# The order of the rows and the cut of the stores in a pairwise outer-product kernel with batch normalisation

## The chip, the cores and the metric

The kernel runs on one core of one Trainium2 chip, alone. The metric is the device time of one execution in microseconds (us). All data are float32. A kernel of this chip writes instructions for several engines, each of which works through its own list in order: PE (TensorE, matmuls), DVE (VectorE), ACT (ScalarE), POOL (GpSimd) and SP (SyncE, which here only issues transfers). Transfers between the device memory (HBM) and the on-chip memory (SBUF, 128 partitions) are carried by 16 DMA engines that take them in the order of issue. Engines wait for each other and for transfers by semaphores.

## The reference: what is computed

There are 1024 samples, 39 fields and 16 values per field. For each pair of fields (r, c) with c < r, 741 pairs in all, the outer product of field r of xj with field c of xi is formed, normalised over the batch, and weighted:

```python
cross = xj[:, rows, :, None] * xi[:, cols, None, :]          # 1024 x 741 x 16 x 16
mean = jnp.mean(cross, axis=(0, 2, 3), keepdims=True)
var = jnp.mean(jnp.square(cross - mean), axis=(0, 2, 3), keepdims=True)
normed = (cross - mean) * jax.lax.rsqrt(var + BN_EPS)
normed = normed * gamma[None, :, None, None] + beta[None, :, None, None]
out = normed[:, :, None, :, :] * W[None, None, :, :, :]
```

The pairs stand in the order of `tril_indices`: row r holds the r pairs (r, 0) to (r, r-1). The inputs are small (5.1 MB). The output is 1024 x 741 x 256 values, 776.99 MB, and all of it must be written.

## The kernel before, in words

**Layout.** Each of the 128 partitions holds eight samples. A tile is one row r for T = 2 of these eight samples, so each row has four tiles (t0 = 0, 2, 4, 6). In the buffer `y_sb` one pair of one sample takes 256 values, 1 KB per partition. `y_sb` has room for 152 such places, that is two halves of 76. A row r from 20 to 37 and its partner 38 - r fill one half together, r pairs for two samples and then 38 - r pairs for two samples; row 38 fills one alone; row 19 fills half of one. Inside a tile the first sample's pairs come first, then the second's (`view`, L135). "Sample 0" and "sample 1" below are these two. Successive halves of work go to the two halves of the buffer in turn (`slot`, L68 to L74), so a half is overwritten by the half after next.

**Order.** The list `tiles` (L67 to L74) fixes the order of the work: four tiles of row 19, then for r = 20, 21, ... 37 the tiles r and 38 - r in turn for the four values of t0, and at the end the four tiles of row 38. Tile number n below is the place in this list: n = 0 to 3 are row 19, 4 to 11 are rows 20 and 18.

**Statistics.** The first 33 us or so load the inputs and work out a scale and a shift for each pair. They are then spread to all partitions by matmuls (`spread`, L475, matmuls at L482), group of rows by group of rows into banks of PSUM, and joined with gamma and beta by three or four small DVE operations per group (`apply`, L491 to L500). ROW_GROUPS (L32) lists for each group its rows, its bank and the tile n after which it is applied. All matmuls are issued before the main loop.

**Main loop (L516).** For tile n: POOL scales xi for tile n + 2 (`scale_xi`, L161; L167); `finish(n)`; the groups that are due; `products(n + 1)`. `products` (L175) writes the raw products of a tile with one instruction per sample and value i of 16: sample 0's sixteen first, then sample 1's. Eleven or twelve of each sixteen are ACT's (L145), the other four or five POOL's (L147). Rows up to SHORT = 4 are made by DVE (L180, L190) from a copy of xj in PSUM, `xj_short`, that ACT makes once (L526). Each product writes all pairs of its sample, so no pair is complete before the last of them. `finish` (L247) then adds the shift and multiplies by W: one DVE instruction per pair for both samples (L284), while for some pairs POOL does it (L270, L273); in rows over LONG = 33 that is eight pairs, and ACT does the addition for them (L268).

**Stores.** `finish` calls `store` (L203) after each piece of pairs that `bounds` (L240) gives: one piece for rows up to ONE = 24, two of r//2 and r - r//2 pairs for longer ones, and a written-out list for the first eight tiles. A store is issued by SP, which waits for the engines that finish the pairs. For a row over ONE the last piece goes out as two stores, one per sample; every other store takes both samples. In each partition a store moves one contiguous run per sample. Rows 25 to 38 thus have three stores per tile, the first of which takes the first half of the pairs of both samples.

Of the kernel before, what the change touches and what calls it, by code (L numbers as in the profile page):

```python
# [14 lines left out]
T = 2  # L15


ONE, LONG = 24, 33
FIRST_PIECES = (
    (0, 1, 3, 6, 10, 14, 19), (0, 4, 9, 14, 19), (0, 4, 11, 19), (0, 9, 19), (0, 10, 20), (0, 9, 18), (0, 10, 20), (0, 9, 18)  # L20
)
# [8 lines left out]


ROW_GROUPS = (  # L32
    (19, 20, 0, None), (20, 21, 1, None), (15, 19, 1, 2), (21, 25, 2, 4), (1, 15, 2, 8), (25, 32, 3, 16), (32, 39, 4, 24)
)
SHORT_GROUP = 4


@with_exitstack
def tile_pair_outer_batchnorm(
# [17 lines left out]
    NB, F, E = xi.shape  # L57
# [8 lines left out]
    mid = (F - 1) // 2  # L66
    tiles = [(mid, t0, t0 // T * half // 2) for t0 in range(0, NT, T)]  # L67
    slot = 0  # L68
    for r in range(mid + 1, F):
        for t0 in range(0, NT, T):  # L70
            tiles.append((r, t0, slot * half))
            if r < F - 1:
                tiles.append((F - 1 - r, t0, slot * half + T * r))
            slot ^= 1  # L74
# [60 lines left out]
    def view(n):  # L135
        r, _, u = tiles[n]
        return y_sb[:, u : u + T * r, :].rearrange("p (t n) e -> p t n e", t=T)
# [23 lines left out]
    def scale_xi(n):  # L161
        r, t0, _ = tiles[n]
        if r <= SHORT:
            return
        n0 = first[r]
        xs = scaled.tile([P, T, r, E], F32, tag="xs", name=f"xs_{r}_{t0}")
        nc.gpsimd.tensor_tensor(  # L167
            xs,
            xi_sb[:, t0 : t0 + T, 0:r, :],
            s_sb[:, :, n0 : n0 + r, :].to_broadcast([P, T, r, E]),  # L170
            ALU.mult,
        )
        xs_of[n] = xs

    def products(n):  # L175

        r, t0, _ = tiles[n]
        if r <= SHORT:
            xs = scaled_short.tile([P, T, r, E], F32, tag="xs_short", name=f"xs_{r}_{t0}")
            nc.vector.tensor_tensor(  # L180
                xs,
                xi_sb[:, t0 : t0 + T, 0:r, :],
                s_short[:, first[r] : first[r] + r]
                .unsqueeze(1)
                .unsqueeze(3)
                .to_broadcast([P, T, r, E]),
                ALU.mult,
            )
            for t in range(T):
                nc.vector.tensor_tensor(  # L190
                    view(n)[:, t].rearrange("p n (i j) -> p n i j", j=E),
                    xs[:, t].unsqueeze(2).to_broadcast([P, r, E, E]),
                    xj_short[:, t0 + t, r - 1 : r, :].unsqueeze(3).to_broadcast([P, r, E, E]),
                    ALU.mult,
                )
            return
        xs = xs_of.pop(n)
        split = E - (POOL_I_FIRST[n] if n < 3 else POOL_I_LONG if tiles[n][0] > LONG else POOL_I)
        for t in range(T):
            for i in range(E):  # L200
                product(n, nc.scalar if i < split else nc.gpsimd, t, i, xs[:, t])

    def store(n, c0, c1, t_from=0, t_to=T):  # L203
        r, t0, _ = tiles[n]
        n0 = first[r]

        step = 1 if r > ONE and c1 == r else t_to - t_from
        for t in range(t_from, t_to, step):
            nc.sync.dma_start(  # L209
                out_v[:, t0 + t : t0 + t + step, (n0 + c0) * EE : (n0 + c1) * EE],  # L210
                view(n)[:, t : t + step, c0:c1, :].rearrange("p t n e -> p t (n e)"),
            )
# [14 lines left out]
    def weigh(n):  # L227

        y = view(n)
        for c0, c1 in zip(bounds(n), bounds(n)[1:]):  # L230
            affine(n, range(c0, min(c1, OWN)), (nc.vector,))
            nc.vector.tensor_tensor(  # L232
                y[:, :, c0:c1, :],
                y[:, :, c0:c1, :],
                w_dve.unsqueeze(1).to_broadcast([P, T, c1 - c0, EE]),
                ALU.mult,
            )
            store(n, c0, c1)
# [8 lines left out]
    def finish(n):  # L247


        r = tiles[n][0]  # L250
        n0 = first[r]
        y = view(n)
        long = r > LONG
        p1 = r // 2 if long else r
        if long:
            share = POOL_PAIRS_LONG
        elif RAW < n < 10:
            share = POOL_PAIRS_FIRST
        else:
            share = int(r * POOL_SHARE + 0.5) if r > SHORT else 0  # L260
        p0 = p1 - share
        step = POOL_PAIRS_LONG // 2 if long else r
        for c0 in range(p0, p1, step):
            c1 = min(c0 + step, p1)
            for c in range(c0, c1):
                t_c = t_sb[:, n0 + c : n0 + c + 1]
                if long:
                    nc.scalar.activation(y[:, :, c, :], y[:, :, c, :], AF.Identity, bias=t_c)  # L268
                else:
                    nc.gpsimd.tensor_scalar(  # L270
                        y[:, :, c, :], y[:, :, c, :], t_c, 1.0, ALU.add, ALU.mult
                    )
            nc.gpsimd.tensor_tensor(  # L273
                y[:, :, c0:c1, :],
                y[:, :, c0:c1, :],
                w_sb.unsqueeze(1).to_broadcast([P, T, c1 - c0, EE]),
                ALU.mult,
            )

        size = 1 if n == RAW else T  # L280
        for t in range(0, T, size):
            for c0, c1 in zip(bounds(n), bounds(n)[1:]):
                for c in [*range(c0, min(c1, p0)), *range(max(c0, p1), c1)]:
                    stt(  # L284
                        y[:, t : t + size, c, :],
                        y[:, t : t + size, c, :],
                        t_sb[:, n0 + c : n0 + c + 1],
                        w_dve.to_broadcast([P, size, EE]),
                        ALU.add,
                        ALU.mult,  # L290
                    )
                store(n, c0, c1, t, t + size)

    with tc.manual_schedule():
# [180 lines left out]
        def spread(group):  # L475
            r0, r1, bank, _ = ROW_GROUPS[group]
            n0, n1 = first[r0], first[r1 - 1] + r1 - 1
            at = used[bank]
            used[bank] = at + 2 * (n1 - n0)
            ps = ps_st[bank][:, at : used[bank]].rearrange("p (x n) -> p x n", x=2)  # L480
            for r in range(r0, r1):
                nc.tensor.matmul(  # L482
                    ps[:, :, first[r] - n0 : first[r] - n0 + r],
                    pick[:, r, :],
                    stq[:, :, 0:r],
                    start=True,
                    stop=True,
                )
            spread_of.append((ps, n0, n1))

        def apply(group):  # L491
            ps, n0, n1 = spread_of[group]
            nc.vector.tensor_mul(ps[:, 1], ps[:, 1], st_sb[:, 0, n0:n1])
            if group == SHORT_GROUP:

                nc.vector.tensor_mul(ps[:, 0], ps[:, 0], st_sb[:, 0, n0:n1])
                nc.vector.tensor_copy(st_sb[:, 0, n0:n1], ps[:, 0])
            else:
                nc.vector.tensor_mul(st_sb[:, 0, n0:n1], ps[:, 0], st_sb[:, 0, n0:n1])
            nc.vector.tensor_add(st_sb[:, 1, n0:n1], ps[:, 1], st_sb[:, 1, n0:n1])  # L500
# [8 lines left out]
        for group in range(1, len(ROW_GROUPS)):  # L509
            spread(group)  # L510
        s_short = spread_of[SHORT_GROUP][0][:, 0]
        apply(1)
# [3 lines left out]
        for n in range(1, len(tiles)):  # L516
            if n + 2 < len(tiles):
                scale_xi(n + 2)
            finish(n)
            for group, (_, _, _, tile_of) in enumerate(ROW_GROUPS):  # L520
                if n == tile_of:
                    apply(group)
            if n + 1 < len(tiles):
                products(n + 1)
            if n == 32:
                nc.scalar.copy(xj_short, xj_sb[:, :, 1 : SHORT + 1, :])  # L526


# [26 lines left out]
```

## Time and profile before

| What | Value |
|---|---|
| median of 4 runs | 1881.72 us (1881.56 to 1882.32) |
| the profiled execution's own time | 1881.62 us |
| its span, first to last instruction | 1879.9 us |
| DVE busy | 1720.5 us (92%) |
| ACT busy | 1642.8 us (87%) |
| POOL busy | 1535.2 us (82%) |
| PE busy | 26.0 us (1%) |
| bytes written to HBM | 776.99 MB |
| stores issued at L209 | 283, from 35.9 to 1862.4 us |
| median us from a store's issue to its landing | 17.2 |

The profile comes from one execution. Busy time is the time in which an engine executes; issuing a transfer and waiting for a semaphore do not count. The page cuts the span in 40 slices of 47 us and shows each engine's busy share as a digit (9 is 90% or more), beside the mean busy share of the 16 DMA engines and the GB/s that they moved. A packet is one piece that a DMA engine moves at a time; a run of a store is one packet here. Rows of instruction groups give line, engine, operation, output and input with their shapes, the count, the busy time and the mean ns of one. Instructions of one engine overlap somewhat, so that a run of many takes less than their count by the mean of one; stretches in the timeline show the time that a run of them took. Waits are given as: who waited <- for whom: us in total, times, longest. Beside these views the trace holds, for every store, when it was issued and when it landed (its last byte reported as written), and for every packet its size and how long it took.

### The profile page before, as it was taken

What the parts mean: (1) busy time and instruction counts of PE and PEld (TensorE: products, weight loads), DVE (VectorE), ACT (ScalarE), POOL (GpSimd) and SP (SyncE); (2) the same over time, 40 slices, a digit from 0 to 9 for tenths busy, and PEclk for the clock granted to TensorE, in tenths of its full rate; (3) what the DMA queues carried; (4) which work ended last, traced back from release to release, by engine and by line L of the source; (5) the groups of instructions that cost most, each with busy time, mean ns of one, the idle gap of its engine ahead of it and who ended that gap; (6) DMA issues with size and microseconds to landing.
All of it is one profiled execution on the core that took longest, in us unless ns stands there. A gap on an engine that the chain in (4) does not pass through costs nothing. (4 is left out here: it accounts for less than half of the span.)

```text
span 1879.9 us, 9660 instructions
## 1 busy us (share of the span) xinstructions
PE 26.0 (1%) x130; PEld 23.3 (1%) x130; DVE 1720.5 (92%) x2625; ACT 1642.8 (87%) x3416; POOL 1535.2 (82%) x1746
## 2 busy tenths in 40 slices
PE   4000000000000000000000000000000000000000
PEld 4000000000000000000000000000000000000000
DVE  8999999998989898989898989898999999988885
ACT  7998989898989798989898989898988888888883
POOL 8999888888888788888888878787888777777873
DMA  5999999999999999999999999999999999999999
GB/s 199 385 421 425 430 426 430 427 427 424 425 427 424 424 425 426 425 424 424 424 423 428 423 425 423 416 425 421 423 419 424 424 423 422 424 419 415 425 415 411
DMA packets 63994, 783.63 MB, mean 417 GB/s; under 512 B 4784, under 2 KB 6448, under 8 KB 17072
## 3 DMA queue, kind: packets, MB, share of 16 engines
q1 hardware_dynamic: 62624, 779.72, 98.3%
q10 hardware_dynamic: 1296, 3.29, 0.5%
q14 instruction: 73, 0.60, 0.1%
q8 instruction: 1, 0.02, 0.0%
HBM read 6.00 MB, written 776.99 MB: 417 GB/s over the span
## 5 line engine op out<-in xcount | busy, mean ns | idle before, releaser
L284 DVE SCALAR_TENSOR_TENSOR y_sb<-y_sb,st_sb,w_dve 128x512 f32<-128x512 f32 (+1 forms) x2511 | 1651.1, 738 | 132.3 <-issue 119.5
L145 ACT ACTIVATE y_sb<-xs,xj_sb 128x288 f32<-128x288 f32 (+20 forms) x3194 | 1510.7, 566 | 193.1 <-DMA out_dram<-y_sb 164.7
L147 POOL TENSOR_SCALAR y_sb<-xs,xj_sb 128x416 f32<-128x416 f32 (+29 forms) x1126 | 607.1, 565 | 40.4 <-DMA out_dram<-y_sb 28.0
L273 POOL TENSOR_TENSOR y_sb<-y_sb,w_sb 128x2048 f32<-128x2048 f32 (+3 forms) x155 | 517.3, 3343 | 103.7 <-ACT y_sb L268 94.1
L167 POOL TENSOR_TENSOR xs<-xi_sb,st_sb 128x640 f32<-128x640 f32 (+33 forms) x135 | 184.2, 1365 | 169.1 <-ACT y_sb L145 162.9
L270 POOL TENSOR_SCALAR y_sb<-y_sb,st_sb 128x512 f32<-128x512 f32 x291 | 197.7, 696 | 0.1
L268 ACT ACTIVATE y_sb<-y_sb,st_sb 128x512 f32<-128x512 f32 x160 | 100.2, 709 | 1.9
L190 DVE TENSOR_TENSOR y_sb<-xs,ps 128x1024 f32<-128x1024 f32 (+3 forms) x32 | 24.8, 817 | 0.5
L482 PE MATMUL ps<-y_sb 39*128 39x38 f32 (+37 forms) x76 | 16.5, 398 | 2.8 <-DVE y_sb L468 2.8
L482 PEld LDWEIGHTS ps<-y_sb 39*128 39x128 f32 x76 | 16.3, 329 | 3.1 <-DVE y_sb L468 3.1
L346 ACT ACTIVATE y_sb<-y_sb 128x1248 f32<-128x1248 f32 x8 | 9.9, 1243 | 2.8 <-POOL y_sb L335 2.8
L351 DVE TENSOR_REDUCE y_sb<-y_sb 128x78 f32<-128x1248 f32 x8 | 11.2, 1446 | 0.4 <-ACT y_sb L346 0.4
L145 ACT ACTIVATE y_sb<-xi_sb,xj_sb 128x304 f32<-128x304 f32 x24 | 11.4, 535 | 0.0
L335 POOL TENSOR_TENSOR y_sb<-xi_sb,y_sb 128x1248 f32<-128x1248 f32 x4 | 9.2, 2322 | 2.3 <-ACT y_sb L384 2.3
L232 DVE TENSOR_TENSOR y_sb<-y_sb,w_dve 128x2048 f32<-128x2048 f32 (+4 forms) x6 | 10.7, 1837 | 0.1
L325 DVE TENSOR_REDUCE y_sb<-xi_sb 128x39 f32<-128x624 f32 (+1 forms) x6 | 6.1, 1012 | 3.8 <-DMA xi_sb<-in_r_xi_dram 3.8
L335 POOL TENSOR_TENSOR y_sb<-xj_sb,y_sb 128x1248 f32<-128x1248 f32 x4 | 9.2, 2321 | 0.0
L371 PE MATMUL ps<-y_sb 128*39 128x79 f32 x48 | 8.1, 340 | 15.4 <-DVE y_sb L351 15.2
L225 POOL TENSOR_SCALAR y_sb<-y_sb,st_sb 128x512 f32<-128x512 f32 x8 | 6.5, 818 | 2.1 <-ACT y_sb L145 2.1
L325 DVE TENSOR_REDUCE y_sb<-xj_sb 128x39 f32<-128x624 f32 (+1 forms) x6 | 6.1, 1014 | 0.6 <-DMA xj_sb<-in_r_xj_dram 0.6
L223 ACT ACTIVATE y_sb<-y_sb,st_sb 128x512 f32<-128x512 f32 x9 | 6.5, 804 | 0.2 <-ACT y_sb L145 0.2
L371 PEld LDWEIGHTS ps<-y_sb 128*39 128x39 f32 x48 | 5.8, 178 | 17.4 <-DVE y_sb L351 10.6
(59 smaller groups left out, 35.2 us busy)
## 6 DMA issues: line engine op xcount, KB each, us to landing
out_dram<-y_sb SPq DMA_DIRECT2D x25, 2304.0 KB, 14.6
out_dram<-y_sb SPq DMA_DIRECT2D x12, 4352.0 KB, 15.4
out_dram<-y_sb SPq DMA_DIRECT2D x12, 4096.0 KB, 16.3
out_dram<-y_sb SPq DMA_DIRECT2D x10, 4608.0 KB, 14.7
out_dram<-y_sb SPq DMA_DIRECT2D x12, 3840.0 KB, 17.5
out_dram<-y_sb SPq DMA_DIRECT2D x21, 2048.0 KB, 17.0
out_dram<-y_sb SPq DMA_DIRECT2D x12, 3584.0 KB, 18.1
out_dram<-y_sb SPq DMA_DIRECT2D x12, 3328.0 KB, 18.1
```

Of the source, the lines that this page charges most:

```text
L145: nc.scalar.activation(y, src, AF.Copy, scale=scale)
L147: engine.tensor_scalar(y, src, scale, 1.0, ALU.mult, ALU.mult)
L167: nc.gpsimd.tensor_tensor(xs, xi_sb[:, t0 : t0 + T, 0:r, :], s_sb[:, :, n0 : n0 + r, :].to_broadcast([P, T, r, E]), ALU.mult,)
L190: nc.vector.tensor_tensor(view(n)[:, t].rearrange("p n (i j) -> p n i j", j=E), xs[:, t].unsqueeze(2).to_broadcast([P, r, E, E]), xj_short ...
L268: nc.scalar.activation(y[:, :, c, :], y[:, :, c, :], AF.Identity, bias=t_c)
L270: nc.gpsimd.tensor_scalar(y[:, :, c, :], y[:, :, c, :], t_c, 1.0, ALU.add, ALU.mult)
L273: nc.gpsimd.tensor_tensor(y[:, :, c0:c1, :], y[:, :, c0:c1, :], w_sb.unsqueeze(1).to_broadcast([P, T, c1 - c0, EE]), ALU.mult,)
L284: stt(y[:, t : t + size, c, :], y[:, t : t + size, c, :], t_sb[:, n0 + c : n0 + c + 1], w_dve.to_broadcast([P, size, EE]), ALU.add, ALU.mult,)
L325: nc.vector.tensor_reduce(total[:, t0:t1, part(x)], sources[x][:, t0:t1], AX.X, ALU.add)
L335: nc.gpsimd.tensor_tensor(devs[n % 7], sources[x][:, t0 : t0 + T], shift[:, x : x + 1, :].unsqueeze(3).to_broadcast([P, T, F, E]), ALU.sub ...
L371: nc.tensor.matmul(ps_g[acc][0:F, 0 : 2 * F + 1], lhs, fb[:, t], start=t == 0, stop=t == NT - 1)
L482: nc.tensor.matmul(ps[:, :, first[r] - n0 : first[r] - n0 + r], pick[:, r, :], stq[:, :, 0:r], start=True, stop=True,)
```

## The change

The change has four parts.

1. The rows come in another order: after rows 19 and 20|18 comes row 38, and then 37|1, 36|2 and so on down to 21|17.
2. ONE becomes 30, so rows 25 to 30 have one piece and not two.
3. From the ninth tile on, rows over 19 are stored by sample. Rows to 30 have two stores, one whole run of r pairs per sample. Rows 31 to 38 have two stores for sample 0, the first r//2 pairs and the rest, and one whole run for sample 1, issued with the last piece. In the first eight tiles the last piece of row 20 is cut by sample too.
4. The groups of the statistics follow the new order: twelve and not seven, with their banks and due tiles; the copy `xj_short` is made after tile 12 instead of tile 32, and SHORT_GROUP names the group of rows 1 to 4.

The instructions that compute the output, their shapes and their engines stay as they are for each tile.

```diff
-ONE, LONG = 24, 33
+ONE, LONG = 30, 33
...
 ROW_GROUPS = (
-    (19, 20, 0, None), (20, 21, 1, None), (15, 19, 1, 2), (21, 25, 2, 4), (1, 15, 2, 8), (25, 32, 3, 16), (32, 39, 4, 24)
+    (19, 20, 0, None), (20, 21, 1, None), (18, 19, 1, 2), (38, 39, 1, 8), (34, 38, 1, 9), (1, 5, 1, 10), (29, 34, 2, 36),
+    (5, 10, 2, 37), (25, 29, 3, 76), (10, 14, 3, 77), (21, 25, 4, 108), (14, 18, 4, 109),
 )
-SHORT_GROUP = 4
+SHORT_GROUP = 5
...
-    for r in range(mid + 1, F):
+    for r in (mid + 1, *range(F - 1, mid + 1, -1)):
         for t0 in range(0, NT, T):
             tiles.append((r, t0, slot * half))
...
-        step = 1 if r > ONE and c1 == r else t_to - t_from
+        whole = n >= len(FIRST_PIECES)
+        step = 1 if r > mid and (whole or c1 == r) else t_to - t_from
         for t in range(t_from, t_to, step):
+            if whole and step == 1 and t == t_to - 1:
+                if c1 < r:
+                    continue
+                c0 = 0
             nc.sync.dma_start(
...
-            if n == 32:
+            if n == 12:
                 nc.scalar.copy(xj_short, xj_sb[:, :, 1 : SHORT + 1, :])
```

## The prediction, made before the changed kernel was built

> **What bounds the kernel.** I read the page's slices first, then its queue line, then busy time by stage, then who waits, and last the trace's records of single stores and packets.
>
> ```profile
> DMA  5999999999999999999999999999999999999999
> GB/s 199 385 421 425 430 426 430 427 427 424 425 427 424 424 425 426 425 424 424 424 423 428 423 425 423 416 425 421 423 419 424 424 423 422 424 419 415 425 415 411
> ...
> q1 hardware_dynamic: 62624, 779.72, 98.3%
> ```
>
> From the third slice on the DMA engines are full and the rate hardly moves. Below, the last two columns are their busy share and GB/s: start-up, 20|18, rows 21-24, 25-30, 31-37, 38.
>
> ```profile
> 36.00:91.00 55.00, 13.68 (x64) 13.47 (x64) 54.27 (x91) 55.00 (x123) 52.80 (x69) 1.00 0.90 366
> 91.00:180.00 89.00, 0.00 (x0) 0.00 (x0) 88.48 (x140) 86.24 (x198) 86.75 (x110) 1.00 1.00 423
> 190.00:540.00 350.00, 0.00 (x0) 0.00 (x0) 330.17 (x504) 317.85 (x720) 293.49 (x375) 1.00 1.00 427
> 560.00:1150.00 590.00, 0.00 (x0) 0.00 (x0) 544.81 (x827) 532.11 (x1204) 489.37 (x628) 1.00 1.01 425
> 1150.00:1745.00 595.00, 0.00 (x0) 0.00 (x0) 548.29 (x833) 510.79 (x936) 475.84 (x452) 1.00 1.00 422
> 1755.00:1860.00 105.00, 0.00 (x0) 0.00 (x0) 90.20 (x140) 81.41 (x120) 76.51 (x52) 1.00 0.99 421
> ```
>
> The share is 1.00 from 91 us; DVE, the busiest engine, rests 6 to 14% after 190 us. The waits agree: ACT waits for stores.
>
> ```profile
> ACT y_sb L145 <- DMA out_dram<-y_sb: 164.7, 66, 4.7
> ```
>
> So the kernel is bound by the store queue. The trace's issue and landing of each store say it more sharply. A half (38 pairs, two samples) is 9.961 MB, a row with its partner four halves. Rows 21 to 24 land in 93.52, 93.53, 93.62 and 93.59 us, mean 93.57; rows 25 to 30 in 94.58, 93.97, 94.45, 93.75, 94.66 and 93.92, mean 94.22; rows 31 to 37 in 94.21 on average; row 38 in 93.47. After 130 us the shortest lead of an issue over the landing before it is 1.48 us. A store on an empty queue (issued at 68.06, landed at 73.91, 1.84 MB, 4.3 us at 427 GB/s) needs about 1.5 us beside its bytes, so the queue never ran dry.
>
> **1. Packets, the gain.** Each stored run is one packet. Per long tile, rows 25-30 had 2 samples x 2 pieces x 128 = 512 and get 256; rows 31-38 get 384. Removed: 24 x 256 + 32 x 128 = 10,240 packets, 640 for each of 16 engines. Three readings of one packet's price:
> - The median packet takes 46 ns at 1,024 bytes, 352 at 9,216, 691 at 18,432 and 916 at 24,576: a line of 8.2 ns plus 27.1 bytes per ns. 640 x 8.2 ns = 5.2 us.
> - Rows 25-30 against 21-24, same bytes, 1,024 packets more: 0.65 us, or 10 x 0.65 = 6.5 us in all.
> - The same with row 26, whose four halves agree within 0.06 us: 0.40, or 4.0 us.
>
> The dearer rows also have 16 stores where 21-24 have 8. Were the price per store, nothing would be won: stores go from 283 to 279 (24 fewer in rows 25-30, 20 more in rows 20-24). But row 38, with 12 stores, lands in 93.47. I take **5.2 us**, the one direct duration, with 0 and 6.5 as ends.
>
> [...]
>
> **2. Order and later stores, the danger.** Before, a store of the first pieces of both samples goes out with DVE half done. Now a row to 30 stores nothing until its DVE work ends, and a longer one sends a quarter of the tile first. In return sample 0 comes free first. Prices, from these rows:
>
> ```profile
> 1660.89 15.05 ACT L145 ACTIVATE y_sb<-xs,xj_sb 128x592 f32<-128x592 f32 x22 [3.33 <-DMA out_dram<-y_sb]
> ...
> 1770.87 19.84 DVE L284 SCALAR_TENSOR_TENSOR y_sb<-y_sb,st_sb,w_dve 128x512 f32<-128x512 f32 x30 [2.95 <-ACT y_sb L145]
> ...
> 1778.88 15.34 ACT L145 ACTIVATE y_sb<-xs,xj_sb 128x608 f32<-128x608 f32 x22 [2.99 <-DVE y_sb L284]
> ```
>
> DVE: 19.84 / 30 = 0.661 us a pair. ACT: 15.34 / 22 = 0.697 a product of row 38. The wait at 1660.89 ended when the first sample's last store landed (1660.73), though the second sample's landed only at 1666.35: waits go by the region of a sample, which this change relies on. Descending rows keep it so: sample 0 of row r-1 lies inside sample 0 of row r.
>
> Count from the landing of sample 1. ACT does that sample's products, DVE all pairs, the store is issued and needs 1.5 us; meanwhile the queue has the partner and the other half, 23.4 us. Row 30: 0.1 + 7.1 (12 x 0.593) + 17.2 (26 x 0.661) + 1.5 = 25.9; the queue lasts 4.9 + 23.4 = 28.3, spare **2.4 us**. From row 31 the quarter piece adds its own time: row 33 spares 3.0, 36 2.6, 37 1.2. Row 38: 0.1 + 7.7 + 19.84 + 1.5 = 29.1 against 23.4 + 5.8 = 29.2, spare **0.1**. Its quarter piece waits for POOL's pairs (issued 11.7 us after DVE's start at 1770.87) and spares 2.3. Rows 21-29 have 3.8 and more.
>
> Entry into row 38 is the one place where a layout changes badly: its sample 1 (pairs 38 to 75) covers the last of 20's and all of 18's, so it waits for the 18-store that lands at 162.48 in this trace. 162.6 + 7.7 puts DVE's start at 170.4, when the 18 before it is done (its store goes at 169.96). The rest of the first 38 is issued at 190.2 and ready at 191.7; the queue lasts until 186.25 + 5.8 = 192.1. It fits by 0.3. I charge **0.4 us** for both (ends 0 and 1.5): here the lead is as thin as the reading.
>
> **3. What else moves.** Statistics: three DVE operations of 0.17 to 0.36 us for each of 12 groups, not 7 (one has four). Up to tile 11 they took some 2.4 us and now take 2.7 (the 66- and 90-column ones go later, 142 and 38 come earlier); DVE works without rest there, but the queue is full from 91 us, so this only eats the 0.3 at the entry. Later ones (155 columns, about 0.9 us) stand against spares of 2.4 and more. The matmuls of L482 run from 33.19 for 16.49 us; those sharing row 20's bank are now 12 rows with row 19, done at 33.2 + 12 x 0.43 = 38.4, before the group is applied at 46.68. The copy of xj_short moves to tile 12: 512 elements, 0.7 us by the ACT rows of that size. Behind it on ACT stand tile 13's eight additions, POOL and the quarter piece wait for those, and they have 2.3 us: nothing; without that spare, 0.7 once. SP issues two stores where there was one at 0.38 us each and else waits for DVE: nothing. The end stays: last landing 1878.83 of a 1879.9 span; then the 17 is issued 9.9 us (15 x 0.661) behind the 21, whose bytes take 12.9. Start-up to 91 us is the same but for 0.15 us of shorter statistics.
>
> **Sum:** -5.2 + 0.4 = -4.8 us. The profiled execution took 1881.62 around a span of 1879.9; the median of four runs is 1881.72. 1881.72 - 4.8 = **1876.9**, or 0.26% less. About 0.2% (3.76 us, 1877.96) is what a measurement of this kernel can tell from no change, so the forecast stands close to it.
>
> **Rivals.**
> - *Packet cost not regained (0.18).* Half the surplus of rows 25-37 sits in single halves of 23.9 to 24.2 us beside quiet ones of 23.4, near packets that fetch instructions; these stay. If runs of 13 KB cost little beyond that, 0 to 3 us are won: 1879 to 1881.7. For it: rows 26 and 28 are within 0.4 us of rows 21-24. Against: the line through the packets.
> - *The lead is lost (0.08), the slower side.* Each loop of two halves loses what DVE starts later than the spare: two loops a row, so 2 x (delay - spare). A delay of 1.5 us costs rows 38 and 37 3.4 us (1880.3); from **2.7 us** on the losses pass 9 us and the kernel is slower by over 0.2%. If ACT waited for a whole tile, some 7 us, rows 28 to 38 would lose about 86 us: 1963. The wait at 1660.89 speaks against it. 0.05 of this case lies above 1885.5, 0.03 below.
> - *More than the packets (0.04).* The earlier start also takes the slow halves away (24.2 once a row): 1872 to 1875.
> - *The forecast (0.70):* 4.0 to 6.5 us, less 0 to 0.8: 1875.2 to 1878.5; 0.07 of it lies above 1877.96.
>
> Faster: 0.63 + 0.04 = 0.67. Same: 0.18 + 0.07 + 0.03 = 0.28. Slower: 0.05. The range runs from 1874.6 to 1881.0: below it most of the third rival, above it the slower one and the top of the first.
>
> **What would show it.** The queue line near 52,300 packets; rows 25-30 landing in about 93.6 us, 31-37 in 93.9; the share still 1.00 between 180 and 280 us, where 38 now stands. A share under 0.98 there, or ACT's wait starting only at the second sample's landing, would prove the second rival; the same packets gone and rows still at 94.2, the first.

## The result and the profile after

The changed kernel takes 1879.5 us (median of 41 runs, 1878.93 to 1880.71) against 1881.61 us of the kernel before (61 runs, 1880.98 to 1882.54). The ratio is 0.9989, with a 95% interval of [0.9985, 0.9993]: 2.1 us faster, 0.11%. The interval does not hold 1, and yet the change is within the 0.2% that the prediction counted as no change, and less than half of the 4.8 us that it forecast. The forecast was 1876.9; the time lies inside the stated range, outside the forecast's own one.

The profiled execution took 1879.32 us, with a span of 1877.6. First the slices and the queue line of its page, as they were shown of before:

```profile
DMA  5999999999999999999999999999999999999998
GB/s 200 385 420 424 405 424 425 424 430 424 425 429 425 425 427 426 426 426 425 421 425 424 433 424 432 425 426 430 425 430 425 429 430 425 432 426 427 427 428 353
...
q1 hardware_dynamic: 52320, 779.72, 97.9%
```

The 10,304 packets less are the 10,240 runs and 64 small ones that belong to four stores. The fifth slice (188 to 235 us) moves 405 GB/s where its neighbours move 424; before, that slice had 430. From the 21st slice to the last but one, 424 to 433 stand where 415 to 428 stood. The last slice fell from 411 to 353; that is taken up below the account. The windows say the same; the last two columns are again the busy share of the DMA engines and GB/s. The stages are now start-up, 20|18, 38, 37 to 31, 30 to 25, and the last four rows.

```profile
36.00:91.00 55.00, 13.46 (x64) 13.31 (x63) 54.19 (x91) 55.00 (x122) 52.88 (x70) 1.00 0.91 369
91.00:180.00 89.00, 0.00 (x0) 0.00 (x0) 85.59 (x139) 85.69 (x178) 87.43 (x100) 1.00 1.01 424
180.00:280.00 100.00, 0.00 (x0) 0.00 (x0) 85.91 (x131) 86.88 (x129) 79.16 (x55) 1.00 0.97 417
280.00:935.00 655.00, 0.00 (x0) 0.00 (x0) 611.68 (x936) 570.08 (x1075) 528.02 (x522) 1.00 1.00 425
940.00:1495.00 555.00, 0.00 (x0) 0.00 (x0) 522.50 (x800) 505.95 (x1148) 466.36 (x597) 1.00 1.00 427
1500.00:1860.00 360.00, 0.00 (x0) 0.00 (x0) 327.66 (x495) 305.54 (x696) 286.08 (x365) 1.00 1.00 428
```

From 91 to 1860 us the queue is full everywhere but in row 38: 0.97 there, the share below 0.98 that the prediction had named as the sign of a lost lead. By landings, the account is:

| Stage | before, us | after, us | difference over all its rows |
|---|---|---|---|
| last landing of row 19 | 91.73 | 91.45 | -0.3 |
| row 20 with 18 | 94.52 | 94.58 | +0.1 |
| row 38 | 93.47 | 96.51 | **+3.0** |
| rows 31 to 37, mean of a row | 94.21 | 93.84 | -2.6 |
| rows 25 to 30, mean of a row | 94.22 | 93.72 | -3.0 |
| rows 21 to 24, mean of a row | 93.57 | 93.75 | +0.7 |
| last landing | 1878.83 | 1876.70 | -2.1 |

Rows 25 to 37 gained 5.7 us; row 38 alone gave 3.0 back. The single stores show where: the rest of the first 38's sample 0 was issued at 192.62 us, when everything issued before it had landed at 191.75. By the measure of the prediction (a store has to be issued 1.5 us before the landing of the one before it) the queue stood dry for 2.4 us there, and for 0.5 us once more at 239.70. The timelines of DVE, POOL and ACT at that place (start, us, engine, line, what, count, idle before and its releaser):

```profile
159.80 10.61 DVE L291 SCALAR_TENSOR_TENSOR y_sb<-y_sb,st_sb,w_dve 128x512 f32<-128x512 f32 x16
172.75 19.84 DVE L291 SCALAR_TENSOR_TENSOR y_sb<-y_sb,st_sb,w_dve 128x512 f32<-128x512 f32 x30 [2.33 <-POOL y_sb L149]
```

```profile
159.17 2.27 POOL L169 TENSOR_TENSOR xs<-xi_sb,st_sb 128x1216 f32<-128x1216 f32 x1
161.42 1.36 POOL L277 TENSOR_SCALAR y_sb<-y_sb,st_sb 128x512 f32<-128x512 f32 x2
162.86 2.37 POOL L280 TENSOR_TENSOR y_sb<-y_sb,w_sb 128x1024 f32<-128x1024 f32 x1
165.19 7.52 POOL L149 TENSOR_SCALAR y_sb<-xs,xj_sb 128x608 f32<-128x608 f32 x10
```

```profile
162.69 7.74 ACT L147 ACTIVATE y_sb<-xs,xj_sb 128x608 f32<-128x608 f32 x11 [0.99 <-DMA out_dram<-y_sb]
```

ACT has its part of row 38's products done at 170.43, as predicted (170.4), and DVE the 18 before it at 170.41 (169.96 in the kernel before). But POOL begins its ten products only at 165.19, behind the scaling of the next 38 and the last two pairs of the 18, and ends them at 172.71. DVE starts 2.35 us later than predicted, and everything of that tile with it.

The end of the kernel changed its form too. The last stretch before, then after:

```profile
1860.00:1879.90 19.90, 0.00 (x0) 0.00 (x0) 2.00 (x4) 0.00 (x0) 0.00 (x0) 1.00 0.92 391
```

```profile
1860.00:1877.60 17.60, 0.00 (x0) 0.00 (x0) 0.00 (x0) 0.00 (x0) 0.00 (x0) 1.00 0.52 224
```

The trace records the landing of a store in 16 steps, as many as there are DMA engines, and the store has landed with the last. The last store of before had all its steps between 1878.67 and 1878.83 us. That of the change had twelve between 1868.62 and 1868.80 and the other four at 1871.02, 1873.09, 1874.30 and 1876.70. The trace does not name the engine of a step, but the reading at hand is that twelve engines were done 8 us before the slowest, and that the kernel ends with the slowest. All landings in this document are last steps, and so is the dry time.

### The profile page after: what moved, and what is told of

The parts are those of the page before. It is cut to its first block, busy times and chain, and to the rows that moved or that the text cites. A ratio compares the mean times of both kernels' runs of the same rounds, so it can differ in the third digit from the quotient of the medians.

```text
span 1877.6 us, 9638 instructions
## 1 busy us (share of the span) xinstructions
PE 26.0 (1%) x130; PEld 23.4 (1%) x130; DVE 1723.8 (92%) x2640; ACT 1645.6 (88%) x3416; POOL 1535.8 (82%) x1746
## 4 chain that ended last, share of the span: by engine, by line
DMA 56%; ACT 19%; DVE 18%; issue 2%; POOL 2%; SPq 0%; ACTq 0%; DVEq 0%; PE 0%; POOLq 0%
DMA out_dram<-y_sb 56%; ACT y_sb L147 19%; DVE y_sb L291 17%; POOL y_sb L149 1%; DVE y_sb L358 1%; POOL xs L169 0%; ACT y_sb L230 0%; DVE y_sb L332 0%; SPq L216 0%; DMA xi_sb<-in_r_xi_dram 0%; POOL y_sb L277 0%; POOL y_sb L280 0%; POOL y_sb L342 0%; DVE y_sb L192 0%; DVE xs L182 0%
## 5 line engine op out<-in xcount | busy, mean ns | idle before, releaser
L149 POOL TENSOR_SCALAR y_sb<-xs,xj_sb 128x480 f32<-128x480 f32 (+27 forms) x1126 | 607.1, 565 | 14.2 <-DMA out_dram<-y_sb 14.1
L192 DVE TENSOR_TENSOR y_sb<-xs,ps 128x256 f32<-128x256 f32 (+3 forms) x32 | 24.8, 818 | 0.6
L378 PE MATMUL ps<-y_sb 128*39 128x79 f32 x48 | 8.1, 340 | 15.3 <-DVE y_sb L358 15.1
(59 smaller groups left out, 37.4 us busy)
```

What stands on the lines that cost most here:

```text
L149: engine.tensor_scalar(y, src, scale, 1.0, ALU.mult, ALU.mult)
L192: nc.vector.tensor_tensor(view(n)[:, t].rearrange("p n (i j) -> p n i j", j=E), xs[:, t].unsqueeze(2).to_broadcast([P, r, E, E]), xj_short ...
L378: nc.tensor.matmul(ps_g[acc][0:F, 0 : 2 * F + 1], lhs, fb[:, t], start=t == 0, stop=t == NT - 1)
```

## The experiments

Each experiment was timed beside the kernel before on the same chip. The kernel before had a median of 1881.43 us beside the first three, 1881.8 beside the next four and 1881.52 beside the last three. "Dry" is the sum over all stores after 125 us of 1.5 us less the lead, where the lead over the landing before is under 1.5, in the profiled execution. That one execution can lie up to 0.7 us beside the median (row 38 after row 24).

| Run | Median, us | Ratio to before [95%] | Difference, us | Dry, us | Difference less dry |
|---|---|---|---|---|---|
| the change | 1879.5 | 0.9989 [0.9985, 0.9993] | -2.1 | 2.9 | -5.0 |
| stores alone | 1918.79 | 1.0198 [1.0184, 1.0212] | +37.4 | 41.7 | -4.3 |
| order alone | 1881.72 | 1.0001 [0.9993, 1.0010] | +0.3 | 0.1 | +0.2 |
| old pieces at the entry | 1878.29 | 0.9983 [0.9974, 0.9992] | -3.1 | 1.9 | -5.0 |
| POOL relieved at the entry | 1877.69 | 0.9979 [0.9970, 0.9988] | -4.1 | 1.4 | -5.5 |
| row 38 after row 24 | 1877.53 | 0.9977 [0.9968, 0.9985] | -4.3 | 0.9 | -5.2 |
| halves cut | 1897.89 | 1.0084 [1.0070, 1.0097] | +16.1 | 0 | +16.1 |
| samples cut | 1880.12 | 0.9992 [0.9983, 1.0001] | -1.7 | 0 | -1.7 |
| row 38 late, in old pieces | 1877.81 | 0.9980 [0.9971, 0.9989] | -3.7 | 1.5 | -5.2 |
| the same, short tiles cut by sample | 1879.65 | 0.9990 [0.9981, 0.9998] | -1.9 | 1.6 | -3.4 |
| program shifted | 1881.49 | 0.9999 [0.9990, 1.0008] | 0.0 | 0 | 0.0 |

**The change taken apart: stores alone.** The order, the groups and the tile of the xj_short copy are those of before, the stores those of the change. Of these edits against the change only the line of the order is shown:

```diff
-    for r in (mid + 1, *range(F - 1, mid + 1, -1)):
+    for r in range(mid + 1, F):
```

> The changed stores alone, with the order of rows and the groups of before. Theory (the descending order is what lets sample 0 start early): going up, sample 0 of row r+1 covers sample 1's first pair of row r, so at each row change all products wait for the last landing, some 7 us later than inside a row; the queue runs dry by 7 less the row's spare, once per row from 28 on, 40 us in all; less 5 to 6 us of packets: about 1916 us. Rival (order does not matter, the saved packets do): 1876 us, and no loss at the entry into row 38.

Measured 1918.79, 2.8 us beside the theory and 43 from the rival. Its trace at the change from row 37 to row 38, ACT:

```profile
1791.73 15.33 ACT L146 ACTIVATE y_sb<-xs,xj_sb 128x608 f32<-128x608 f32 x22 [10.87 <-DMA out_dram<-y_sb]
```

Row 37's second sample landed at 1791.63, its first at 1780.46. ACT waited 10.87 us, for the second, and then did the products of both samples in one go; in the descending order those of the first would have been done by then. The next store was issued 3.54 us after the queue's last landing. Row by row the landings exceed 93.6 us about as the formula 7 less the spare has it: row 38 by 7.4 us (formula 6.9), 37 by 6.2 (5.8), 36 by 4.8 (4.4), 33 by 4.8 (4.0), 30 by 4.2 (4.6), 28 by 1.5 (1.8, with the spare worked out like those of the prediction).

**Order alone.** The order and the groups are those of the change, ONE is 24 and `step` is that of before.

> The changed order and groups alone, with the stores of before. Theory (the entry into row 38 loses only because its first store is a quarter tile of 5.8 us; a half tile of 11.6 us covers the late rest): no packets saved and no loss, 1881.0 to 1881.8. Rival (row 38 that early loses 3 us whatever is stored, since POOL is late there): 1884 to 1885.

Measured 1881.72 beside 1881.43, no difference. Row 38 lands in 94.01 us although DVE was late there too: its first store, a half of both samples, was issued at 184.86 and kept the queue busy until 198.00, and the next one, issued at 193.04, had 5 us of lead. So the lateness of POOL costs nothing behind a store of 11.6 us, and 2.4 us behind one of 5.8.

**Old pieces at the entry.** Only tile 12 differs from the change.

```diff
-        whole = n >= len(FIRST_PIECES)
+        whole = n >= len(FIRST_PIECES) and n != 12
```

> The changed kernel, but the first tile of row 38 (tile 12) is stored in the pieces of before: the first half of both samples (11.6 us), then one store per sample; 128 packets more. Theory: the 2.2 us that the queue stood dry before the landing at 199.83 are gone, 1877.0 to 1877.8. Rival (the loss of row 38 is not the dry queue at the entry): 1879.5.

Measured 1878.29: half of it. The dry place at the entry is gone (the rest of the first 38 has a lead of 5.04 us). But the quarter piece is what lets sample 0 go early: it now landed at 203.20 instead of 199.83. ACT did both samples of tile 14 in one go from 203.31, and came to the second some 1.2 us after that had come free at 209.78 (an estimate from half of the 15.34 us that the two took). The queue stood dry for 1.9 us at 238.60 instead. Most of the rest of the gain went there.

**POOL relieved at the entry.** The change, with one product per sample of tile 12 and one pair of tile 11 less for POOL.

```diff
-        split = E - (POOL_I_FIRST[n] if n < 3 else POOL_I_LONG if tiles[n][0] > LONG else POOL_I)
+        split = E - (POOL_I_FIRST[n] if n < 3 else POOL_I_LONG if tiles[n][0] > LONG and n != 12 else POOL_I)
...
+        elif n == 11:
+            share = 1
         else:
             share = int(r * POOL_SHARE + 0.5) if r > SHORT else 0
```

> The changed kernel with POOL relieved at the entry into row 38: tile 12 gives POOL 4 of 16 products per sample, not 5, and tile 11 (the 18 before it) 1 pair, not 2. Theory (DVE waited there for POOL until 172.75): POOL, ACT and DVE are then all ready near 171.1, the first 38 starts 1.6 us earlier and the queue stands dry 1.6 us less: about 1878 us. Rival (the wait for the landing of the 18 sets the start): 1879.5.

Measured 1877.69. DVE and POOL at the entry, to be held against the two fences above:

```profile
170.96 19.84 DVE L293 SCALAR_TENSOR_TENSOR y_sb<-y_sb,st_sb,w_dve 128x512 f32<-128x512 f32 x30 [0.18 <-issue]
```

```profile
163.07 6.00 POOL L149 TENSOR_SCALAR y_sb<-xs,xj_sb 128x608 f32<-128x608 f32 x8
```

POOL ends at 169.07, DVE starts at 170.96 with 0.18 us of idle time, 1.8 us earlier than in the change, and the kernel is 1.8 us faster. Row 38 lands in 94.98 instead of 96.51. That the landing of the 18 sets the start, the rival, is out: it landed at about the same time in both (162.4 and 162.6).

**Row 38 after row 24.** The stores of the change, the groups of before, another order.

```diff
-    for r in (mid + 1, *range(F - 1, mid + 1, -1)):
+    for r in (*range(mid + 1, 25), *range(F - 1, 24, -1)):
```

> The changed stores with another order: 19, 20 up to 24 with their partners, then 38 down to 25; groups of before. Row 38 then comes where DVE, ACT and POOL rest and the queue has a full lead. Theory (the loss of 3 us in row 38 came from its place, where no engine had reserve): no dry queue at its entry, 1876.3 to 1877.2. Rival (row 38's own loop is too long for its quarter piece wherever it stands): 1878.3 or more.

Measured 1877.53, the lowest median, though its runs (1876.92 to 1878.99) overlap those of POOL relieved; it is 0.3 us above the expected range. At this entry DVE starts when ACT's last products of the tile are done, at 546.80, and POOL had ended its own at 542.89. DVE, ACT and POOL:

```profile
546.89 19.84 DVE L290 SCALAR_TENSOR_TENSOR y_sb<-y_sb,st_sb,w_dve 128x512 f32<-128x512 f32 x30 [7.16 <-issue]
```

```profile
539.79 7.01 ACT L146 ACTIVATE y_sb<-xs,xj_sb 128x608 f32<-128x608 f32 x10
```

```profile
539.88 3.01 POOL L148 TENSOR_SCALAR y_sb<-xs,xj_sb 128x608 f32<-128x608 f32 x4
546.95 2.27 POOL L168 TENSOR_TENSOR xs<-xi_sb,st_sb 128x1216 f32<-128x1216 f32 x1 [4.06 <-ACT y_sb L146]
```

No store comes after the queue has run out; three in row 38 miss the lead of 1.5 us by 0.2 to 0.5. That is row 38's own loop, which the prediction gave a spare of 0.1: the place cost 2.4 us, the loop under 1.

**The price of a packet: halves cut and samples cut.** Both are the kernel before with the stores of rows 2 to 24 cut in two, 84 stores more. One cuts the pairs, so that there are 21,504 packets more; the other cuts by sample, with not one packet more (apart from 16 small ones that go with every store).

```diff
+        if n >= len(FIRST_PIECES) and 1 < r <= ONE and c1 - c0 == r:
+            store(n, 0, r // 2)
+            store(n, r // 2, r)
+            return
```

```diff
-        step = 1 if r > ONE and c1 == r else t_to - t_from
+        cut = n >= len(FIRST_PIECES) and 1 < r <= ONE
+        step = 1 if cut or r > ONE and c1 == r else t_to - t_from
```

> The kernel before with the stores of its rows 2 to 24 (84 tiles from the ninth on) cut in two, the first half of the pairs of both samples and the second half, issued together: 84 stores and 21,504 packets more (1,344 per engine). Theory (packets cost): 1,344 x 8.2 to 9.3 ns = 11.0 to 12.5 us, 1892.5 to 1894 us. Rival (the pieces of before cost through something else): under 3 us, below 1884.5.

> The control to the run with cut halves: the same 84 stores of before cut in two by sample, so 84 stores more and not one packet more. Theory (packets cost, stores do not): 1881.2 to 1882 us. Rival (the price is one per store): as much as the run with cut halves.

Halves cut: 1897.89; samples cut: 1880.12. The stores cost nothing that shows; the packets cost 17.8 us against the control and 16.1 against the kernel before, 13.2 or 12.0 ns each on every engine, more than the theory's 8.2 to 9.3. Their rates, slice by slice, first halves, then samples:

```profile
GB/s 202 385 420 420 422 421 421 420 422 423 420 421 421 420 423 421 421 420 423 421 421 420 422 422 421 420 416 417 420 419 416 420 416 416 415 420 415 423 419 408
```

```profile
GB/s 198 385 422 426 430 427 430 427 426 432 426 426 424 426 425 423 425 424 425 424 424 426 423 424 420 419 418 418 420 426 420 425 425 426 417 425 423 424 424 411
```

By rows, rows 21 to 24, with runs of 7 to 12 KB, land in 95.19 against 93.95 us for 2,048 packets more: 9.7 ns. Rows 25 to 36, where the cut runs are those of the partners, 1 to 7 KB, land in 95.06 against 94.08 for 1,024 more: 15.3 ns. But against the kernel before, the same rows give 12.7 ns (95.19 against 93.57) and 13.2 (95.06 against 94.22). So that shorter runs cost more is not shown. That all cut runs cost more than the line through the packets has it is shown; why, stays open.

**Two attempts at more.** Row 38 late, in the pieces of before; then also all short tiles by sample.

```diff
-        whole = n >= len(FIRST_PIECES)
-        step = 1 if r > mid and (whole or c1 == r) else t_to - t_from
+        whole = n >= len(FIRST_PIECES) and r < F - 1
+        step = 1 if whole or r > mid and c1 == r else t_to - t_from
```

(The second changed line belongs to the second run alone.)

> The run with row 38 after row 24, and row 38 itself stored in the pieces of before (first half of both samples, then one store per sample); 512 packets more than that run. Theory (what is left between it and the forecast is the 0.9 us that the queue stood dry in row 38's loop): 0.9 less dry time, 0.3 us more of packets, so 0.6 us faster: 4.8 us under the kernel before, 1876.5 to 1877.2. Rival (row 38's dry time is the loop's, whatever the piece): no faster than before this edit, 1877.5.

> As the run before it, and the short tiles' stores cut by sample too: 84 stores more, no packet more. Theory (the 1.7 us that cutting by sample won in the kernel before came from the stores' shape): 1.7 us faster than the run before it, 1875 us. Rival (it was an accident of that program, such as where its instruction fetches fell): the same time as the run before it, within 0.7 us.

Measured 1877.81 and 1879.65. Row 38 itself ran without a dry place (93.29 us), but row 37 behind it took 95.22: with the old pieces sample 0 of row 38 goes later, and the first 37 stood dry for 1.2 us. So the first theory missed: the dry time moved one row on. Cutting the short tiles by sample, 1.7 us to the good in the kernel before with an interval that holds 1, was 1.8 us to the bad here; its theory fell.

**Program shifted.** 64 copies of one element on ACT, where it waits.

```diff
+            if 20 <= n < 84:
+                nc.scalar.copy(spare, spare)
             if n == 32:
```

> The kernel before with 64 copies of one element per partition on ACT, one behind the products of each tile from 20 to 83, where ACT waits for stores anyway. It leaves stores, packets and order as they are and moves the places at which later instructions are fetched. Theory (the slow halves are packets of instructions that fall on the slowest of the 16 engines, so shifting the program moves the total by a hit or more): 0.6 to 2 us away from the kernel before, either side. Rival (the slow halves belong to the order and the stores): within 0.4 us.

Measured 1881.49 beside 1881.52. The slow halves of 23.9 to 24.2 us did move (row 36's from its first half to its last), but the total did not. So this one shift gives no sign that the places of the fetches make differences of 1 to 2 us; that no other shift does is not shown, and what the two runs with cut samples changed beside their stores is not known.

## Why the prediction was right, and where it was not

- **What bounds the kernel: right.** Stores are always waiting (a DMA share of 1.00 from 280 to 1860 us), except where the queue runs dry (0.97 in row 38), and those places with the packets make most of the differences between the runs. The prediction went by one landing per store and so did not see how far its 16 steps drift apart: up to 5.3 us before (the store that landed at 1183.09) and 8.3 after (at 1843.32).
- **Packets, 5.2 us: right, with a doubt on the size.** The last column of the table gives 5.0 to 5.5 us in five runs that save those packets and let sample 0 go early, which is 7.8 to 8.6 ns for each of 608 to 640 packets per engine; the packets' line had 8.2. The stores alone give 4.3, from a dry sum of 41.7, and the run with short tiles cut by sample 3.4. Samples cut moved the time by 1.7 us the one way and 1.8 the other without a packet, for a reason not known, so a single 5 us holds to some 2 us. The halves cut, at 12.0 to 13.2 ns a packet, cost more than the line has; joining runs of 12 KB and more paid. The count of stores was free to within those 1.7 us: samples cut.
- **Waits by the region of a sample, and the loop's spare: right**, and shown by the stores alone (there ACT waited 10.87 us, until row 37's second sample had landed). The prediction priced the second rival by 2 x (delay - spare) per row. That run delays one loop per row by some 7 us, and the same sum gave 40 us, measured 41.7 dry. Row 38's spare of 0.1 was right to half a microsecond (leads of 1.00 and 1.59 against 1.5).
- **The entry into row 38: wrong.** "It fits by 0.3" had ACT, DVE and the landing of the 18, each right to 0.5 us, and left out POOL. The prediction had POOL's duties in row 38 from that row's loop at the end of the kernel before, where POOL rests (76.51 of 105 us busy); between 91 and 180 us it worked 86.75 of 89 us before, and its list puts the next scaling and the 18's pairs ahead of the products. With them, 159.17 + 2.27 + 1.36 + 2.37 + 7.52 gives 172.7, 2.3 us behind ACT. The 0.4 us charged for order became 2.9: that is nearly the whole distance from 1876.9 to 1879.5. The upper end of the charge, 1.5, was too low.
- **The rivals.** The time fell where the first rival (packet cost not regained) was placed, but by the second one's mechanism at one place: the packets paid in full and a lost lead took half of it. The share of 0.97 between 180 and 280 us was the sign set down for that. That 1879.5 still lies in the stated range is luck: its upper part was there for the first rival, and a loss that the prediction left out filled it.
- **The rest: right but for the end.** DVE ended the 18 0.45 us later, as the larger statistics there have it, and waited for POOL anyway. The copy of xj_short took 0.57 us at 193.75 and the piece behind it had 6.0 us of lead. The last landing is 0.9 us before the span's end, as before (1.1). But "the end stays" missed the twelve steps that are done 8 us early: by last landings that costs nothing, and it is time in which, by the reading above, most of the engines stand idle (a DMA share of 0.52 after 1860 us).
- **Not tested:** 0.7 us more in rows 21 to 24, of which one half of 24.12 us in row 23 is most. In that half the last step of the landings fell back by another 0.7 us at 1666.4, with two packets that fetch instructions at 1656.7 and 1657.1.

## What to carry to other kernels

When transfers bound a kernel, cutting them finer to free buffers and cutting them coarser to save packets are one decision (here 5.0 us won in packets, 2.9 lost to a dry queue): what the queue still holds when the next piece is due has to be counted for every engine that has a part in that piece, with the work that stands ahead of it in that engine's list at that place, and not with durations from a calmer stage. A piece stored first should last as long as the rest needs (at the entry into row 38 one of 11.6 us did, one of 5.8 did not), and a tile with the thinnest lead belongs where all engines rest: the same stores were worth 2.1 us with row 38 at 170 us and 4.3 with it at 547. The order in which a buffer is refilled decides whether fine stores help at all: without the descending rows these cost 37 us. And a store has landed only with the last of its 16 steps, which at the end of the change came 8 us behind the twelfth, so the spread of its steps is worth a look beside its landing.

## What the runs showed of the hardware that was not expected

- A packet's cost on a full queue was 7.8 to 8.6 ns where runs of 12 to 19 KB were joined and 12.0 to 13.2 where runs of 2 to 24 KB were cut, while the line through the packets' own durations has one intercept, 8.2 ns.
- The landings of halves jump between 23.0, 23.4 and 24.2 us although stores are queued. Slow ones stand near packets that fetch instructions (73 of 8 KB in the kernel before). After 130 us the last step of a landing fell back by over 0.5 us behind the mean of the first twelve 15 times before and 13 times after, by up to 1.3 us, and each time such a packet (0.31 us by itself) had started after the first step of the landing before, or up to 1 us ahead of it. A program shifted by 64 instructions changes which halves are slow, but its time by 0.03 us.
- A store issued on an empty queue took 1.5 us beside its bytes (before: 68.06 to 73.91 us, 4.3 of them for 1.84 MB). Measured by that one number, the dry sum brought six of the seven runs with those packets saved, from 1877.5 to 1918.8 us, to within 0.7 us of one gain of 5 us; the seventh, with short tiles cut by sample, is 1.6 us off.
